# Giving the depthwise filters to an instruction order in units of five or three rounds instead of one

## The chip, the cores and the metric

The kernel runs on one NeuronCore of a Trainium2 chip. The metric is the device time in microseconds of one execution of the whole kernel (lower is better); the time of a kernel is the median of several executions.

## The reference

Four layers run one after the other on x of shape (32, 56, 56, 96), float32, images in the first dimension and channels last.

- Layer 0 makes per-image mixing weights of four experts (`rw = sigmoid(mean(x) @ Wr + br)`), expands 96 channels to 384 with a mixed 1x1 product, normalisation and relu, filters each of the 384 channels with a mixed 3x3 filter (again normalised, relu), projects to 96 channels, and adds the input.
- Layer 1 filters each of the 96 channels with its own 5x5 filter and adds the result to its input:

```
y = conv(x, kernel5x5, groups=96, padding='SAME')
x = x + y
```

- Layer 2 applies relu, then filters each channel with its own 3x3 filter, then takes a 96x96 product over channels with a bias and a normalisation:

```
y = relu(x)
y = conv(y, dw_kernel3x3, groups=96, padding='SAME') + dw_bias
y = (y @ pw_kernel + pw_bias) * inv + (beta - moving_mean * inv)
```

- Layer 3 is a Swin block: attention in shifted 7x7 windows (three heads of 32), with layer norm ahead, and a perceptron of width 384 with a second layer norm, each added to its input.

## The kernel before, in words

**Stages.** Each image passes through four stages: `stage_router` (layer 0's mixing weights), `stage_conditional` (the rest of layer 0), `stage_depthwise` (layers 1 and 2) and `stage_swin` (layer 3). In step s of the outer loop the stages of four images are recorded together: the router of image s, the conditional stage of s-1, the depthwise stage of s-2 and the Swin stage of s-3.

**Where the order comes from.** The stages are generators. They do not issue instructions; they record them as units of work (`Work`), one for each call on the recorder `chip`, or one for all calls inside a `with chip.together()` block. A generator's `yield n` says that n of the stage's total weight has been recorded (49 for the depthwise stage). `interleave` turns this into a due time (`chip.target`) for what follows: the stage's planned start plus its planned length times the share already recorded, with `PLAN["depthwise"] = (1.48, 1.13)` in units of images.

`Recorder.order` then simulates the five queues with a table of costs (`COST` and `cost`). When an engine is free it takes, of the units in its queue, the one with the earliest due time whose buffers are available; units that lack a buffer are passed over. A unit enters its queue when all that it depends on is done. The event that puts it there is handled after the engines were last asked, so when a unit on TensorE ends, its direct successor is not yet in the queue at the moment TensorE chooses again: if anything else can start, that goes first. If TensorE finds nothing for 250 ns, the planner gives it a filler, a product of the identity with itself (`chip.spare`; `banks<-ident` of 128x128 in the profile). The order found is issued as it is, on all engines, by `give`: this is line 500, and so nearly all instructions of the profile carry L500.

**Banks.** All products go to one ring of eight PSUM banks (`mm = cv = banks("banks", 8)`). A unit takes its banks when it starts; a bank comes free when its last user is done. A unit that starts a bank also waits for the buffers that the users of this bank write (for the second half of layer 2 that is `x3`, of which there is one).

**The depthwise stage.** `x1` holds the image as 128 partitions: 32 channels of a group are spread with four rows of the image each (`RB = 4`), three groups (`NG = 3`), and 14 blocks of four rows in the free dimension, padded to 60 columns. Filters are banded 32x32 matrices (`band5`, `band3`), so that a product of 32 rows by 32 columns of TensorE mixes eight channels with four rows each. A *round* is twelve such products, three groups by four quarters, each at its own place in the array. Layer 1 takes ten rounds for each half of the image, two row blocks (m = 0, 1) by five columns (d = 0 to 4); layer 2 takes six for each half, two row blocks by three columns. All rounds of a half add up in three banks. The halves of layer 1, and the first of layer 2, have 7 blocks (392 columns); the second half of layer 2 has 8 (448 columns).

After a half of layer 1, ScalarE writes `x2` from the three banks with relu (`x<-banks` in the profile). After a half of layer 2, ScalarE copies the banks to `x3`, and DMAs bring it into `filtered` in natural order. Then eight units of products with `pw` (`banks<-pw,filtered`) make the tokens of the Swin stage (`res`).

**Other units named below.** `banks<-xT,wmix`: expansions of layer 0. `banks<-h,wmix`: its projections. `h<-h,mix,h`: its filter taps on VectorE. `banks<-ident,lnd`: transposes of normalised tokens in the Swin stage; `lnd` is made by GpSimd, as are `tb` and `var`. `banks<-hT,w` and `banks<-w,hid`: the perceptron's two products. `banks<-exps,ones`, `banks<-exps,v`, `banks<-wo,oT`, `banks<-slots,wq` and the like: attention.

Of the kernel before, what the change touches and what calls it, by code (L numbers as in the profile page):

```python
# [36 lines left out]
NG = 3  # L37
NQ = 4
# [465 lines left out]
def kernel(  # L504
# [82 lines left out]
    for at, name in (  # L587
# [4 lines left out]
        src = a[name]  # L592
        if len(src.shape) == 1:
            src = src.rearrange("(o m) -> o m", o=1)
        elif len(src.shape) == 4:
            src = src.rearrange("e a b m -> (e a b) m")
# [8 lines left out]
    for at, name in (  # L605
# [4 lines left out]
        src = a[name]  # L610
        if len(src.shape) == 1:
            src = src.rearrange("(o m) -> o m", o=1)
        elif len(src.shape) == 4:
            src = src.rearrange("a b o m -> (a b o) m")
# [143 lines left out]
    chip = Recorder(nc)  # L758
# [174 lines left out]
    def stage_depthwise(b, res):  # L933

        def lines(t):

            return t.rearrange("(c r) m w -> c r m w", r=RB)

        x1 = chip.new(x1s)
        x2 = chip.new(x2s).part(0, 1)
        filtered = chip.new(filtereds).part(0, 1)

        xT = added.pop(b).rearrange("c (m r w) -> c r m w", r=RB, w=W)
        for g in range(NG):
            gs = slice(32 * g, 32 * g + 32)
            half = RB // 2
            for to, r, m in ((half, 0, 0), (0, half, 1)):
                for k in range(half):  # L950
                    chip.sync.dma_start(
                        out=lines(x1[:, g, m : m + NBLK, 2 : 2 + W])[:, to + k], in_=xT[gs, r + k]
                    )
        yield 6


        def tiles(banks, weights, src, first, n, dx, back):

            for t in range(2 * dx):
                m, d = divmod(t, dx)  # L960
                with chip.together():
                    for g in range(NG):
                        for q in range(NQ):
                            other = (q - g if back else q + g) % NQ
                            qs, os = slice(32 * q, 32 * q + 32), slice(32 * other, 32 * other + 32)
                            chip.tensor.matmul(
                                banks[g][os, : n * W].rearrange("p (m w) -> p m w", w=W),
                                weights[qs, g, t],
                                src[qs, g, first + m : first + m + n, d : d + W],
                                start=(t == 0),  # L970
                                stop=(t == 2 * dx - 1),
                            )
                yield 1

        for u in range(2):
            banks = [chip.new(cv) for _ in range(NG)]
            n = NBLK // 2
            yield from tiles(banks, band5, x1, n * u, n, 5, False)
            for g in range(NG):
                chip.scalar.activation(  # L980
                    x2[:, g, 1 + n * u : 1 + n * (u + 1), 1 : 1 + W].part(u),
                    banks[g][:, : n * W].rearrange("p (m w) -> p m w", w=W),
                    AF.Relu,
                )


        for first, n in ((0, NBLK // 2), (NBLK // 2, NBLK // 2 + 1)):
            banks = [chip.new(cv) for _ in range(NG)]
            half = int(first > 0)
            yield from tiles(banks, band3, x2.part(*range(half + 1)), first, n, 3, True)  # L990
            x3 = chip.new(x3s)
            for g in range(NG):
                pc = banks[g][:, : n * W].rearrange("p (m w) -> p m w", w=W)
                chip.scalar.copy(x3[:, g, :n, : W - 3], pc[:, :, 3:])
                chip.scalar.copy(x3[:, g, :n, W - 3 :], pc[:, :, :3])
            for g in range(NG):
                gs = slice(32 * g, 32 * g + 32)
                src = lines(x3[:, g])

                m = max(first, 1)  # L1000
                last = min(first + n, NBLK)
                into = filtered.part(half)
                dst = into[gs, RB * (m - 1) : RB * (last - 1)].rearrange("c (m r) w -> c r m w", r=RB)
                for r in range(RB):
                    chip.sync.dma_start(out=dst[:, r], in_=src[:, r, m - first : last - first])
                for r in range(1, RB) if first == 0 else (0,):
                    chip.sync.dma_start(out=into[gs, H - RB + r], in_=src[:, r, 0 if r else NBLK - first])

        for i in range(NROW):
            tokens = filtered.part(*((0,) if i < 3 else (0, 1))).rearrange("c r w -> c (r w)")  # L1010
            pt = chip.new(mm)
            if i % 2 == 0:
                res.append(chip.new(ress))
            into, n = chunk(res, i)
            with chip.together():
                for j in range(n):
                    at = LT * (NL * (i // 2) + i % 2 * 4 + j)
                    chip.tensor.matmul(
                        pt[:LT, j * CM : (j + 1) * CM],
                        tokens[:, at : at + LT],  # L1020
                        pw,
                        start=True,
                        stop=True,
                    )
            chip.scalar.copy(into.rearrange("p j c -> p (j c)"), pt[:LT, : n * CM])
            yield 1
            if i == 2:
                yield 3
# [8 lines left out]
    def chunk(res, i):  # L1037

        return (parts(res, i, 4, NL), NL - 4) if i % 2 else (parts(res, i, 0, 4), 4)
# [527 lines left out]
```

## Time and profile before

| | |
|---|---|
| time, median of 3 runs | 5202.46 us (5202.14 to 5204.24) |
| span of the profiled execution, first to last instruction | 5212.6 us |
| the profiled execution's time outside this span | not given |
| mean granted TensorE clock | 0.985 |
| TensorE matmul records, busy | 58578, 5050.6 us (97%) |
| of these filter products (`banks<-x,band`) | 24576, 856.3 us |
| VectorE busy | 4300.9 us (83%) |
| ScalarE busy | 3836.9 us (74%) |
| GpSimd busy | 3028.8 us (58%) |

PE is TensorE, DVE VectorE, ACT ScalarE, POOL GpSimd, SP the engine that issues the DMAs. A product in float32 is two matmul records, so one round of twelve products appears as 24 records ("x24") and a run of five rounds as x120. In a timeline line the columns are the start, the time from first start to last end, the engine, the line, the operation, its tiles, its shape and the number of records; successive units of the same form are merged. Matmuls are pipelined and the ends are modelled, so the time a unit takes from TensorE is read from its start to the start of the next unit.

### The profile page before, as it was taken

To read this page: it belongs to the slowest core of one execution; us is meant where nothing else is said; L and a number is where in the kernel's file an instruction comes from. 1 tells how busy PE (TensorE), PEld (TensorE's weight loads), DVE (VectorE), ACT (ScalarE), POOL (GpSimd) and SP (SyncE) were. 2 spreads that over 40 slices of the span, in tenths; PEclk is the share of its full clock that TensorE was granted. 3 is DMA by queue.
4 is the path that set the end of the run, shared out by engine and by line. 5 is a ranking of instruction groups with operands and counts; after the bars stand their busy time and mean duration, and the time that the engine had idled before them with its cause. 6 is when DMAs were issued, how large, how long until landed. Compare 5 with 4: busy or idle time off the path is not lost.

```text
span 5212.6 us, 139630 instructions
## 1 busy us (share of the span) xinstructions
PE 5050.6 (97%) x58578; PEld 3343.9 (64%) x58578; DVE 4300.9 (83%) x5561; ACT 3836.9 (74%) x7649; POOL 3028.8 (58%) x2432
## 2 busy tenths in 40 slices
PE   5789999999999999999999999999999999999999
PEld 4556666666666666666666666666666666666677
DVE  7877988888888888888888888888888888888722
ACT  3457778877778777777877777877777877777755
POOL 5455766565665556666555665656576555566533
PEclk9899999999999999999999999999999999999999
DMA  1111101111111111111111111111111111110110
GB/s 43 23 28 37 38 18 32 33 39 36 39 21 30 31 39 36 39 23 30 33 35 37 37 30 26 30 36 38 37 35 22 32 33 39 36 39 21 23 28 19
DMA packets 482577, 166.34 MB, mean 32 GB/s; under 512 B 477951, under 2 KB 478612, under 8 KB 478868
## 3 DMA queue, kind: packets, MB, share of 16 engines
q1 hardware_dynamic: 481940, 157.33, 14.8%
q8 instruction: 463, 7.59, 0.6%
q14 instruction: 174, 1.43, 0.1%
HBM read 41.60 MB, written 38.54 MB: 15 GB/s over the span
## 4 chain that ended last, share of the span: by engine, by line
PE 74%; POOL 10%; DVE 5%; ACT 5%; issue 4%; DMA 1%; SPq 0%; ACTq 0%; DVEq 0%; POOLq 0%
PE banks L500 74%; DVE h L500 3%; POOL tb L500 3%; POOL lnd L500 2%; POOL xT L500 2%; ACT exps L500 2%; POOL exps L500 2%; POOL var L500 1%; ACT hid L500 1%; ACT h L500 1%; DMA out<-tb 1%; DVE wmix L500 1%; DVE hid L500 1%; ACT slots L500 0%; DVE res L500 0%
## 5 line engine op out<-in xcount | busy, mean ns | idle before, releaser
L500 DVE SCALAR_TENSOR_TENSOR h<-h,mix,h 128x784 f32<-128x784 f32 x3072 | 3309.6, 1113 | 71.1 <-ACT h L500 54.0
L500 POOL TENSOR_TENSOR var<-var,mhalf 112x4 f32<-112x4 f32 (+1 forms) x512 | 775.2, 1519 | 426.3 <-DVE var L500 419.6
L500 PE MATMUL banks<-x,band 32*32 32x392 f32 x24576 | 856.3, 510 | 0.0
L500 POOL TENSOR_TENSOR xT<-y,xT 96x392 f32<-96x392 f32 x256 | 470.2, 1838 | 445.5 <-ACT y L500 444.1
L500 PE MATMUL banks<-xT,wmix 96*128 96x448 f32 (+1 forms) x1536 | 697.9, 553 | 0.5 <-DVE wmix L500 0.5
L500 ACT ACTIVATE h<-h,biasd,s 128x784 f32<-128x784 f32 x384 | 398.9, 1039 | 366.1 <-DVE h L500 366.0
L500 ACT ACTIVATE hid<-banks,c 128x448 f32<-128x448 f32 (+1 forms) x768 | 436.5, 582 | 288.3 <-PE banks L500 279.9
L500 POOL TENSOR_TENSOR tb<-res 112x384 f32<-112x384 f32 (+1 forms) x256 | 476.4, 1866 | 286.7 <-DMA out<-tb 196.7
L500 PEld LDWEIGHTS banks<-w,hid 128*112 128x112 f32 x5376 | 584.7, 183 | 82.0 <-issue 37.8
L500 PE MATMUL banks<-hT,w 96*128 96x448 f32 (+1 forms) x1536 | 615.6, 502 | 0.2 <-DVE tb L500 0.2
L500 POOL TENSOR_TENSOR lnd<-res,var 112x384 f32<-112x384 f32 (+1 forms) x512 | 594.8, 1168 | 32.8 <-PE banks L500 16.2
L500 ACT ACTIVATE h<-banks,bias,s 128x448 f32<-128x448 f32 (+1 forms) x768 | 538.6, 709 | 91.0 <-PE banks L500 85.4
L500 PE MATMUL banks<-w,hid 128*112 128x96 f32 x5376 | 593.1, 267 | 7.4 <-ACT hid L500 6.4
L500 PE MATMUL banks<-h,wmix 128*96 128x392 f32 x1536 | 557.7, 501 | 15.7 <-ACT h L500 15.7
L500 PEld LDWEIGHTS banks<-x,band 32*32 32x32 f32 x24576 | 404.7, 103 | 250.9 <-issue 165.9
L500 ACT ACTIVATE exps<-banks 49x196 f32<-49x196 f32 x1536 | 506.2, 330 | 40.2 <-PE banks L500 15.3
L500 POOL TENSOR_TENSOR exps<-exps,keep_column 49x147 f32<-49x147 f32 x224 | 207.1, 925 | 480.8 <-ACT exps L500 427.4
L500 PEld LDWEIGHTS banks<-h,wmix 128*96 128x96 f32 x1536 | 244.1, 165 | 256.8 <-issue 209.2
L500 PEld LDWEIGHTS banks<-xT,wmix 96*128 96x128 f32 x1536 | 261.2, 192 | 200.7 <-issue 95.5
L500 DVE TENSOR_REDUCE var<-lnsq 112x4 f32<-112x388 f32 (+1 forms) x512 | 253.1, 497 | 157.6 <-POOL lnd L500 118.1
L500 ACT ACTIVATE h<-h,mix 128x784 f32<-128x784 f32 x384 | 364.5, 949 | 18.0 <-POOL h L500 10.1
L500 PEld LDWEIGHTS banks<-hT,w 96*128 96x128 f32 x1536 | 256.4, 190 | 144.9 <-issue 74.8
(132 smaller groups left out, 7460.2 us busy)
## 6 DMA issues: line engine op xcount, KB each, us to landing
xT<-in_x SPq DMA_DIRECT2D x32, 1176.0 KB
x<-xT SPq DMA_DIRECT2D x384, 98.0 KB
out<-tb SPq DMA_DIRECT2D x128, 168.0 KB
filtered<-x SPq DMA_DIRECT2D x384, 49.0 KB
filtered<-x SPq DMA_DIRECT2D x384, 42.0 KB
out<-tb SPq DMA_DIRECT2D x128, 126.0 KB
filtered<-x SPq DMA_DIRECT2D x384, 7.0 KB
wpw<-in_L_conv_Wpw SPq DMA_DIRECT2D x1, 576.0 KB
```

The costliest lines, as they stand in the source:

```text
L500: getattr(getattr(self.nc, w.engine), method)(*args, **kw)
```

## The change

`tiles`, the function that records the filter products of one half of an image, no longer closes a unit after each round. It makes one unit for each row block m, holding all its rounds: five for layer 1, three for layer 2 (60 or 36 products). The products, their operands and their sequence are the same. The generator yields 5 or 3 after such a unit where it yielded 1 after each round, so the due times of all that follows are as before; the second and later rounds of a unit come under the due time of its first.

```diff
         def tiles(banks, weights, src, first, n, dx, back):
 
-            for t in range(2 * dx):
-                m, d = divmod(t, dx)
+            for m in range(2):
                 with chip.together():
-                    for g in range(NG):
-                        for q in range(NQ):
-                            other = (q - g if back else q + g) % NQ
-                            qs, os = slice(32 * q, 32 * q + 32), slice(32 * other, 32 * other + 32)
-                            chip.tensor.matmul(
-                                banks[g][os, : n * W].rearrange("p (m w) -> p m w", w=W),
-                                weights[qs, g, t],
-                                src[qs, g, first + m : first + m + n, d : d + W],
-                                start=(t == 0),
-                                stop=(t == 2 * dx - 1),
-                            )
-                yield 1
+                    for t in range(m * dx, (m + 1) * dx):
+                        d = t - m * dx
+                        for g in range(NG):
+                            for q in range(NQ):
+                                other = (q - g if back else q + g) % NQ
+                                qs, os = slice(32 * q, 32 * q + 32), slice(32 * other, 32 * other + 32)
+                                chip.tensor.matmul(
+                                    banks[g][os, : n * W].rearrange("p (m w) -> p m w", w=W),
+                                    weights[qs, g, t],
+                                    src[qs, g, first + m : first + m + n, d : d + W],
+                                    start=(t == 0),
+                                    stop=(t == 2 * dx - 1),
+                                )
+                yield dx
 
         for u in range(2):
             banks = [chip.new(cv) for _ in range(NG)]
```

## The prediction

> **What bounds the kernel now.** I read the page's engine and chain lines first, then TensorE's waits, then the timeline at the places where the filters run.
>
> ```profile
> PE 5050.6 (97%) x58578; PEld 3343.9 (64%) x58578; DVE 4300.9 (83%) x5561; ACT 3836.9 (74%) x7649; POOL 3028.8 (58%) x2432
> PE 74%; POOL 10%; DVE 5%; ACT 5%; issue 4%; DMA 1%; SPq 0%; ACTq 0%; DVEq 0%; POOLq 0%
> PE banks L500 <- POOL lnd L500: 51.3, 45, 2.8
> PE banks L500 <- ACT h L500: 47.4, 16, 5.4
> L500 PE MATMUL banks<-ident 128*128 128x128 f32 x1672 | 242.5, 288 | 39.9 <-ACT h L500 29.0 <-ACT y L500 10.0 <-ACT slots L500 0.4
> ```
>
> TensorE carries 74% of the chain that ended last and idles 3%, a third of it ahead of the first image. The third and fourth lines (total us, times, longest) are the large waits inside the loop. The last line is the planner's filler, an identity product given out when nothing else can start: two records each. Counted by stretches of 155 us it is 20 records an image in the steady part, 10 products of 0.29 us; the rest lies at head and tail. So in steady state TensorE loses about 3 us an image to filler and 2 us to waits: **TensorE's own work sets the pace**, and what counts is how long its units take in the order given.
>
> Now the filter products (a record is half an fp32 product, so one round of 12 is x24):
>
> ```profile
> 2482.90 1.02 PE L500 MATMUL banks<-x,band 32*32 32x448 f32 x24
> 2483.85 1.02 PE L500 MATMUL banks<-xT,wmix 96*128 96x448 f32 x2
> 2484.80 1.02 PE L500 MATMUL banks<-x,band 32*32 32x448 f32 x24
> ...
> 2511.61 14.20 PE L500 MATMUL banks<-x,band 32*32 32x392 f32 x480
> 2525.74 1.02 PE L500 MATMUL banks<-xT,wmix 96*128 96x448 f32 x2
> ...
> 2547.25 2.62 PE L500 MATMUL banks<-x,band 32*32 32x392 f32 x72
> 2549.80 0.49 PE L500 MATMUL banks<-ident,lnd 112*96 112x112 f32 x3
> ...
> 2622.13 0.92 PE L500 MATMUL banks<-xT,wmix 96*128 96x448 f32 x2
> 2622.89 0.91 PE L500 MATMUL banks<-hT,w 96*128 96x448 f32 x2
> ...
> 2676.83 0.83 PE L500 MATMUL banks<-wo,oT 97*112 97x97 f32 x6
> 2677.59 9.93 PE L500 MATMUL banks<-x,band 32*32 32x392 f32 x336
> 2687.45 2.21 PE L500 MATMUL banks<-h,wmix 128*96 128x392 f32 x6
> 2689.59 0.92 PE L500 MATMUL banks<-x,band 32*32 32x392 f32 x24
> ```
>
> Subtract starts. A lone round costs 0.95 us at 8 rows of blocks (448 columns), and 0.85 at 7. Three in a row cost 2.55 (2549.80 - 2547.25), no less than three lone ones. Fourteen cost 9.86, twenty 14.13: 0.70 each. Inside a run the rounds start 0.67 us apart and the last takes 1.20, so **a run of three or more costs 0.67 a round plus 0.55**, a lone one 0.67 plus 0.18. The unit before pays too: an expansion of 448 columns takes 0.76 (2622.89 - 2622.13) ahead of a full-array unit, 0.95 (2484.80 - 2483.85) ahead of a filter round.
>
> In the trace's records I count 468 runs of filter products in 32 images, 415 of them single rounds. In steady state images alternate. An even image has layer 1 as one run of 20, then 4 runs of layer 2's first half (1, 1, 1, 3 rounds) and 6 single rounds of the second: 11 runs. An odd one has layer 1 as 3 single, one of 14, 3 single, then 12 single rounds: 19.
>
> The planner explains this. When a round ends, its successor enters the queue only after TensorE has chosen again, so anything else that can start goes between. In a run of 20 the "anything else" is the other half of layer 1: the halves alternate and hold six of eight banks. The six evacuations x<-banks confirm it: all start from 2525.7 on, after the run. In the odd image the second half got its three banks only after three rounds: 3, then 7+7=14, then 3.
>
> **What the Trainium skill says.** TensorEngine Tiling (Array Packing), Key Properties: changing the tiling mode, not just the tile, drains TensorE. The trace agrees: between full-array units the next starts 0.16 us before the modelled end of the last; around a 32x32 run 0.07. TensorE: Matmul & The Clock Gate, Part 3 (The mechanism) says matmuls start and end in program order[...]. Perfetto Trace Analysis, Optimization Strategy, says repeated gaps can mean too few buffers to start the next tile; the fillers fit this only loosely.
>
> **The change part by part.** The products, weights and their sequence inside an accumulation stay: 24,576 records, the same evacuations, copies and DMAs. Nothing is added on any queue, SP's and POOL's included; the costs of these edits are nothing by count. What changes is that a unit is 60 or 36 products, nothing gets between its rounds, and the later rounds of a unit carry the first one's due time.
>
> 1. *Layer 1, even images.* After the first five rounds the planner stands where it stood after one: the other half is overdue and has its banks, or so I assume. I take the run of 20 as kept: 0. If it falls apart into four: 4 x (5 x 0.67 + 0.55) = 15.5 against 14.1, 1.4 an image worse.
>
> 2. *Layer 1, odd images.* Now 6 x 0.85 + 9.86 = 14.96. After: a five, something else, then fifteen: 3.88 + 10.54 = 14.42. Gain 0.54 x 16 images = 8.7 us. Bounds: 14.1 as one run, 15.5 as four.
>
> 3. *Layer 2.* Three lone rounds 2.55 or 2.83, a unit of three 2.55 or 2.83: nothing in themselves.
>
> 4. *Fewer switches.* After: even 1 + 2 + 2 = 5 runs, odd 2 + 2 + 2 = 6; over 16 pairs 176, so 292 fewer. What the unit ahead pays, from medians with a filter behind against a full-array unit behind: expansion 448 columns 0.18 (91 times), 392 columns 0.18 (31), hT,w 0.17 (59), pw,filtered 0.09 (127; taken from wo,oT, of the same shape), wo,oT 0.09 (42), the rest 0.02 to 0.17. Weighted 0.125 us. 29 of 468 runs are followed by another small mode, where the switch stays: 0.117. **292 x 0.117 = 34 us.**
>
> 5. *Waiting behind a longer unit.* A unit that becomes ready now waits up to 3.9 us in layer 1, 2.5 or 2.8 in layer 2, where it waited under 1 beside lone rounds and 10 to 14 beside the long runs. Behind it are queued the expansions that feed ACT's h and VectorE's taps, and the transposes and products of attention. Cover: even now ACT's only short of work and POOL is busy 0.15 of 14.4 us in the run of 20, and the image's time survives it. I take 0; bounds -1.4 us an image (banks free earlier, half the fillers go) and +2.9 (fillers double).
>
> Sum on TensorE: 34 + 9 = 43 us. It counts where TensorE is on the chain. Over two images (2480 to 2800 us) the chain is 80% TensorE; it lies on ACT and POOL from 2561 to 2591 and on POOL from 2607 to 2626, and the filter runs lie outside both stretches. What is saved before a POOL stretch can return as a longer wait for lnd, though. I credit 85%: 37 us. The durations are those of the profiled execution, whose span, 5212.6, is 10 us over the median of the runs; no other time of that execution is given. 37 of 5212.6 is 0.7%, and 5202.5 - 37 gives **5166**.
>
> **Rivals.**
>
> *No change (about 5206).* Layer 1 falls into four units with others between in every image: even +1.4 and 3 switches more, odd +0.55 and 3 fewer: 16 x 1.95 = +31. Layer 2 alone gives 14 fewer runs a pair: 16 x 14 x 0.117 = -26. Net +5. For it: the planner's rule that a successor is never at hand. Against: two overdue halves fill each other's gap now.
>
> *Slower (about 5246).* The long unit holds TensorE when an attention product or expansion becomes ready; its ACT, VectorE and POOL steps start later, and the image later has nothing for TensorE: fillers and waits for lnd. Price: 10 more fillers an image, 2.9 us, over 30 images 87, less 43 is +44. It decides from 43/30 = 1.4 us an image, five fillers or half a unit of lost time once. For it: POOL's tb, var, lnd stretch already stops TensorE 2.7 us in one image of two, and a new order lands elsewhere in all of these. Against: the run of 20 is a longer block than any unit here.
>
> *Faster still (about 5125).* Layer 2 holds three banks for some 6 us a half where it held them for about 10, and x3 with them; half the fillers go, 1.4 x 30 = 42 us more.
>
> **How the numbers follow.** Main case 0.50, faster still 0.10, no change 0.15, slower 0.25. Differences within 0.2% (10 us) are about what a measurement of this kernel cannot tell from none. Faster 0.60, same 0.15, slower 0.25. The range, 5130 to 5240, leaves out about half of the fastest case and a little of the slow one. For the main case alone: 5145 to 5188.
>
> **What would show it.** x24 runs all but vanish: the filter runs become x72 and x120 or multiples, about 176 of them. A lone x72 costs 2.55 or 2.83, a lone x120 3.88. Expansions are 0.76 more often. The identity row stays near 1672 and waits for lnd near 51 us. I am wrong if layer 1 shows four x120 runs an image (no change), or if fillers and waits rise by over 1.4 us an image (slower).

## The result, and the profile after

The changed kernel takes 5919.14 us (median of 4 runs, 5912.66 to 5926.2) against 5203.2 us before (5202.14 to 5204.24): 716 us more, ratio 1.1376 with a 95% interval of 1.136 to 1.1392. The execution that was profiled took 5912.66 us; its span is 5910.9 us, its mean granted TensorE clock 0.929.

The page of the changed kernel: the engine line, the chain that ended last, VectorE's filter taps, the filter products and the planner's filler (busy us, mean ns of one | idle before, releaser).

```profile
PE 5321.9 (90%) x59518; PEld 3741.5 (63%) x59518; DVE 4205.9 (71%) x5561; ACT 3850.4 (65%) x7649; POOL 3225.6 (55%) x2432
PE 63%; POOL 15%; DVE 9%; issue 9%; ACT 2%; DMA 1%; SPq 0%; POOLq 0%; ACTq 0%; DVEq 0%
L500 DVE SCALAR_TENSOR_TENSOR h<-h,mix,h 128x784 f32<-128x784 f32 x3072 | 3242.3, 1093 | 589.0 <-ACT h L500 581.1
L500 PE MATMUL banks<-x,band 32*32 32x392 f32 x24576 | 777.7, 501 | 5.1 <-issue 3.1
L500 PE MATMUL banks<-ident 128*128 128x128 f32 x2612 | 406.0, 297 | 49.7 <-ACT y L500 25.2
```

TensorE's share of the chain fell from 74% to 63%. Span less TensorE's busy time was 162.0 us before and is 589.0 now: 427 of the 698 us by which the span grew are idle time. The other 271 are busy time: fillers +163.5 (406.0 less 242.5), filter products -78.6 (777.7 against 856.3 us), and some 187 us in which the rest of the same work ran slower. The clock is enough to explain that: (1 - 0.929) x 5910.9 = 420 us of full clock are missing, against (1 - 0.985) x 5212.6 = 78. Laid over TensorE's busy time in the two traces, 315 us of this fall within it now and 69 did before, 245 more; the rest is lost while TensorE idles, where it costs nothing further. VectorE's taps wait 581.1 us for ACT's h now; in the kernel before, the wait was (total us, times, longest):

```profile
DVE h L500 <- ACT h L500: 54.0, 34, 17.3
```

TensorE's waits after (total us, times, longest):

```profile
PE banks L500 <- POOL lnd L500: 429.3, 84, 14.5
PE banks L500 <- ACT h L500: 72.6, 42, 6.2
```

The wait for GpSimd's `lnd` was 51.3 us with a longest of 2.8. It now holds most of the new idle time, in pieces of up to 14.5 us.

TensorE's timeline after, one image (start, us, engine, line, operation and tiles, records, wait ahead):

```profile
2549.11 0.79 PE L500 MATMUL banks<-ident,lnd 112*96 112x112 f32 x3 [3.94 <-POOL lnd L500]
...
2562.73 5.15 PE L500 MATMUL banks<-x,band 32*32 32x448 f32 x144
2567.81 2.40 PE L500 MATMUL banks<-pw,filtered 97*112 97x97 f32 x22
...
2612.17 0.92 PE L500 MATMUL banks<-ident,lnd 112*96 112x112 f32 x4 [5.13 <-POOL lnd L500]
2623.70 0.80 PE L500 MATMUL banks<-ident,lnd 112*96 112x112 f32 x3 [7.07 <-POOL lnd L500]
...
2644.70 16.05 PE L500 MATMUL banks<-x,band 32*32 32x392 f32 x552
2661.10 2.62 PE L500 MATMUL banks<-x,band 32*32 32x392 f32 x72
2663.65 1.04 PE L500 MATMUL banks<-qT,kT 32*113 32x98 f32 x24
...
2678.61 0.31 PE L500 MATMUL banks<-wr,pooled_w 96*128 96x4 f32 x2
```

The filters did bunch, more than predicted: all twenty rounds of layer 1 and three of layer 2 are one run (x552), and the second half of layer 2 is one run of six rounds (x144), now in the middle of the perceptron instead of at its end. Counted in the records, 468 runs became 113. The loss is elsewhere: two waits for `lnd` at the start of the next attention, 12 us together, and one of 3.9 us in the perceptron.

All engines at the second of these waits:

```profile
2612.62 9.54 DVE L500 SCALAR_TENSOR_TENSOR h<-h,mix,h 128x784 f32<-128x784 f32 x10
2612.89 10.13 POOL L500 TENSOR_TENSOR xT<-y,xT 96x392 f32<-96x392 f32 x1
2622.98 0.66 POOL L500 TENSOR_TENSOR lnd<-res,var 112x288 f32<-112x288 f32 x1
2623.70 0.80 PE L500 MATMUL banks<-ident,lnd 112*96 112x112 f32 x3 [7.07 <-POOL lnd L500]
2625.78 1.75 PE L500 MATMUL banks<-xT,wmix 96*128 96x448 f32 x2
2627.47 1.84 PE L500 MATMUL banks<-qT,kT 32*113 32x98 f32 x24
2634.20 1.72 PE L500 MATMUL banks<-xT,wmix 96*128 96x448 f32 x2
2637.70 5.96 DVE L500 SCALAR_TENSOR_TENSOR h<-h,mix,h 128x784 f32<-128x784 f32 x6 [15.54 <-ACT h L500]
```

An add on GpSimd (median 1.4 us over its 256 executions) starts 0.27 us after a row of ten VectorE taps and takes 10.13 us: it ends 0.86 us after the row does. `lnd` stands behind it on GpSimd, the transposes behind `lnd` on TensorE, and behind these, in order, the two expansions that were to feed ACT's h. The first takes 1.69 us to the next start (2627.47 - 2625.78) where one took 0.76 or 0.95 before, since TensorE's clock stands at half from 2619.1 to 2636.2; the second starts only at 2634.20. So VectorE, which held GpSimd up, has no taps for 15.54 us. The Trainium skill, SBUF — State Buffer, Who interferes with whom, states that a VectorE instruction with two SBUF inputs contends with a GpSimd instruction that reads SBUF, and calls the contention an exclusive lock. The trace agrees in kind; here the add waited out the whole row of ten, not one instruction.

DMA traffic, which is high in the first of the windows below, is a rival that the trace rules out. Of the 31 such adds that take over 8 us, all lie under taps for at least 99% of their time, and 6 have next to no DMA beside them; 4 that take under 2 us have a DMA share over 0.4.

Windows over the same stretch (sum, then busy us and count of PE, PEld, DVE, ACT, POOL; granted clock; DMA share; GB/s):

```profile
2601.00:2621.00 20.00, 9.38 (x33) 5.34 (x31) 19.28 (x23) 7.64 (x12) 16.39 (x4) 0.87 0.55 114
2621.00:2641.00 20.00, 17.30 (x123) 12.19 (x125) 4.46 (x6) 11.17 (x26) 7.10 (x7) 0.62 0.00 0
```

In 40 us TensorE idles 13.3 us and loses 0.13 x 20 + 0.38 x 20 = 10.2 us more to the clock. VectorE is full in the first window and nearly empty in the second.

The second change of order is in layer 0. The mixing weights of the next image (the router) need one small TensorE product and then a chain of short VectorE operations. TensorE and VectorE before, at that product and at the last operation of the chain:

```profile
2384.14 0.31 PE L500 MATMUL banks<-wr,pooled_w 96*128 96x4 f32 x2
```

```profile
2416.76 0.27 DVE L500 TENSOR_SCALAR bias<-bias,s,t 96x1 f32<-96x1 f32 x1
```

and VectorE after:

```profile
2740.47 0.29 DVE L500 TENSOR_TENSOR prod<-experts,rw 128x132 f32<-128x132 f32 x1
2741.62 0.28 DVE L500 TENSOR_REDUCE mix<-prod 128x33 f32<-128x132 f32 x1
...
2746.59 0.27 DVE L500 TENSOR_SCALAR bias<-bias,s,t 96x1 f32<-96x1 f32 x1
2746.78 1.02 DVE L500 SCALAR_TENSOR_TENSOR h<-h,mix,h 128x784 f32<-128x784 f32 x1
...
2752.51 10.00 DVE L500 SCALAR_TENSOR_TENSOR h<-h,mix,h 128x784 f32<-128x784 f32 x9 [3.52 <-ACT h L500]
```

Matching the recorded order with the trace gives which image each belongs to. Before, the weights were ready at 2417, the taps of the image ahead ran until 2453, and the next image's began at 2441: stages overlapped by 12 us. After, the input of the small product is ready at 2655.4 and the product runs at 2678.6, behind the filter runs and a row of attention units (23 us, where it waited 7 before). Its VectorE chain then ends at 2746.9, where the last tap of the image ahead begins (2746.78). From the product to that end it takes 68 us, where it took 33 before, so the larger part of the delay arises on VectorE, among the taps. The next image's taps begin at 2753. The stages no longer overlap: 176 us of taps and 5 of gap make 181 us an image, against some 155. Of these 26 us, 17 are the overlap that is gone (12 and 5), and 9 are a longer tap stage (176 us against 163 and 171 in turn).

### The profile page after: what moved, and what is told of

Same layout as the page of the kernel before. It is cut to its first block, busy times and chain, and to the rows that moved or that the text cites. A ratio compares the mean times of both kernels' runs of the same rounds, so it can differ in the third digit from the quotient of the medians.

```text
span 5910.9 us, 141223 instructions
## 1 busy us (share of the span) xinstructions
PE 5321.9 (90%) x59518; PEld 3741.5 (63%) x59518; DVE 4205.9 (71%) x5561; ACT 3850.4 (65%) x7649; POOL 3225.6 (55%) x2432
## 4 chain that ended last, share of the span: by engine, by line
PE 63%; POOL 15%; DVE 9%; issue 9%; ACT 2%; DMA 1%; SPq 0%; POOLq 0%; ACTq 0%; DVEq 0%
PE banks L500 63%; DVE h L500 7%; POOL xT L500 5%; POOL var L500 4%; POOL lnd L500 3%; POOL tb L500 2%; DMA out<-tb 1%; POOL exps L500 1%; ACT h L500 1%; DVE hid L500 1%; DVE tb L500 1%; DVE wmix L500 0%; ACT exps L500 0%; DVE var L500 0%; DVE oT L500 0%
## 5 line engine op out<-in xcount | busy, mean ns | idle before, releaser
L500 DVE SCALAR_TENSOR_TENSOR h<-h,mix,h 128x784 f32<-128x784 f32 x3072 | 3242.3, 1093 | 589.0 <-ACT h L500 581.1
L500 POOL TENSOR_TENSOR xT<-y,xT 96x392 f32<-96x392 f32 x256 | 716.0, 2798 | 405.3 <-ACT y L500 403.1
L500 PE MATMUL banks<-x,band 32*32 32x392 f32 x24576 | 777.7, 501 | 5.1 <-issue 3.1
L500 PE MATMUL banks<-ident,lnd 112*96 112x112 f32 x1792 | 287.7, 286 | 429.3 <-POOL lnd L500 429.3
L500 PEld LDWEIGHTS banks<-x,band 32*32 32x32 f32 x24576 | 544.8, 103 | 174.5 <-issue 79.8
L500 PEld LDWEIGHTS banks<-ident,lnd 112*96 112x96 f32 x1792 | 210.1, 138 | 598.8 <-POOL lnd L500 473.2
L500 POOL TENSOR_TENSOR tb<-res 112x384 f32<-112x384 f32 (+1 forms) x256 | 348.8, 1367 | 375.0 <-DMA out<-tb 234.2
L500 PEld LDWEIGHTS banks<-ident 128*128 128x128 f32 x2612 | 384.8, 212 | 130.1 <-issue 48.6
L500 ACT ACTIVATE slots<-banks,c 96x392 f32<-96x392 f32 (+2 forms) x384 | 208.2, 581 | 384.2 <-PE banks L500 384.0
L500 PE MATMUL banks<-ident 128*128 128x128 f32 x2612 | 406.0, 297 | 49.7 <-ACT y L500 25.2
```

Of the source, the lines that this page charges most:

```text
L500: getattr(getattr(self.nc, w.engine), method)(*args, **kw)
```

## The experiments

Four theories. A: the long units are harmless, the new order is the culprit. B: a long unit blocks TensorE's queue by its length, in any order. C: rows of taps catch GpSimd's instructions, and TensorE waits behind them. D: the router comes too late, and the stages of neighbouring images stop overlapping. Ratios are to the kernel before on the same chip.

**The old order, rounds brought together at issue.** The planner plans single rounds as before. `mates` lists the rounds of one row block; when the first is issued, the others follow at once.

```diff
+    def gathered(self, found):
+        for w in found:
+            mates = getattr(w, "mates", (w,))
+            if w is mates[0]:
+                yield from mates
...
-            for w in self.order():
+            for w in self.gathered(self.order()):
...
+            mates = [], []
...
+                mates[m].append(chip.work[-1])
+                chip.work[-1].mates = mates[m]
```

> The planner works on single rounds as before and its order is kept; only when the order is issued are the five or three rounds of a row block brought together, at the place of the first. Theory A (a new order of the whole kernel is what costs): the units are as long as in the changed kernel but the order round them is the one of before, so the time is 5203 less the saved switches, 5150 to 5190 us, with waits for lnd near 51 us and fillers at 1672 records. Theory B (a long unit in itself starves the other engines): slower than before by hundreds of us, 5450 to 5900, with waits for lnd over 200 us.

5309.41 us, 1.0207 (1.0187 to 1.0226). The records show 175 filter runs, and the units ahead of filters did get cheaper: pw,filtered 201.8 to 185.3 us, hT,w 579.8 to 572.8, xT,wmix, w,hid and wo,oT some 5 us each, 39 in all (from start to start, waits included). Yet the time rose by some 104 us. TensorE's waits in this run, its timeline at one, and the chain of waits into it:

```profile
PE banks L507 <- POOL exps L507: 72.2, 26, 5.7
PE banks L507 <- POOL lnd L507: 58.9, 60, 2.8
```

```profile
2548.54 1.53 PE L507 MATMUL banks<-exps,ones 113*32 113x392 f32 x6 [5.18 <-POOL exps L507]
```

```profile
2537.61 9.74 POOL xT L507
...
2547.43 1.07 POOL exps L507
...
2548.54 58.25 PE banks L507 x916
```

Here `exps` stands behind an add that the taps have held up, 9.74 us. The wait is 5.18 us, and from its middle on TensorE's clock stays at half for 13.65 us. So both expectations failed: long units at their old places are not free, as A expected, nor do they cost hundreds of us, as B did. Of the 716 us this explains 104 at most.

**One layer alone, and due times alone.** The first run has units of five in layer 1 only; the second has units of three in layer 2 (`size = 3 if dx == 3 else 1`); the third keeps single rounds and gives all of a row block the due time of the first (`size = 1`, `yield 0 if (t0 + 1) % dx else dx`).

```diff
-            for t in range(2 * dx):
-                m, d = divmod(t, dx)
+            size = 5 if dx == 5 else 1
+            for t0 in range(0, 2 * dx, size):
                 with chip.together():
+                    for t in range(t0, t0 + size):
+                        m, d = divmod(t, dx)
...
-                yield 1
+                yield size
```

> Units of five for layer 1, single rounds for layer 2. Theory A: part of the loss, 5250 to 5500 us; the two halves of layer 1 no longer alternate with single rounds and the order settles into another cycle. Theory B: most of the loss lies here, since the 3.9 us units are the longest: 5650 or more.

> Single rounds for layer 1, units of three for layer 2. Theory A: part of the loss, 5250 to 5550 us, the more so if it is layer 2's interleaving that kept TensorE in work while VectorE ends a conditional stage. Theory B: little, 5200 to 5300, since units of 2.5 us are short.

> Single rounds as before, but all rounds of a row block come under the due time of its first, as in the changed kernel. Theory A: the order changes by the due times alone, 5230 to 5450 us. Theory B: no unit is longer than before, so 5190 to 5220.

Layer 1 alone: 5438.9 us, 1.0447 (1.0419 to 1.0474). Layer 2 alone: 5673.99, 1.0898 (1.0875 to 1.0921). Due times alone, with not one long unit: 5374.95, 1.0324 (1.0303 to 1.0344). Any of these plans the kernel anew, and each new plan is worse. All three speak against B: units of five rounds cost 233 us, the shorter units of three 468, and single rounds under new due times 169. Layer 2 alone does more harm than layer 1, with its router late in the same way (ready at 2682 while the taps of the image ahead end at 2683).

**The caught add moved.** The add into `xT` is issued on VectorE instead of GpSimd at its old place in the order: in the changed kernel, in the gathered one, and in the kernel before as a control.

```diff
+        self.issuer = None
...
-                    getattr(getattr(self.nc, w.engine), method)(*args, **kw)
+                    getattr(getattr(self.nc, w.issuer or w.engine), method)(*args, **kw)
...
+            chip.work[-1].issuer = "vector"
```

> The changed kernel with its planned order; only when it is issued, the add of y to xT (256 instructions) goes to VectorE's queue in place of GpSimd's. Theory C (a GpSimd instruction that is caught behind a run of VectorE's taps takes some 10 us, the normalised tokens or probabilities that TensorE waits for are queued behind it, and each such wait is followed by microseconds at half clock): in the changed kernel one xT add an image is caught so, so the waits for lnd fall from 429 to under 200 us, the clock that is lost halves, and the time falls to 5500 to 5700 us. It cannot come back to 5203, since the order itself has 940 more filler records. Theory B (long units starve the engines whatever GpSimd does): above 5850.

> The order of before with the rounds of a row block brought together at issue (run e1), and the add of y to xT on VectorE's queue. Theory C: the wait of 5.2 us for exps in one image of two goes (72 us to under 15) and with it its 13.7 us at half clock, so about 100 us come back and the switches saved show at last: 5150 to 5220 us. Theory B: the long units cost by themselves, 5290 or more.

> Control: the kernel before with the same add on VectorE's queue. Only 6 of its 256 xT adds took over 4 us, so theory C expects little: 141 us more work on VectorE, spread, against less on GpSimd; 5150 to 5240 us. If it falls as far as e6 does against e1, the add has nothing to do with the units' length.

Changed: 5941.16 us, 1.1434 (1.1395 to 1.1473). Gathered: 5410.46, 1.0397 (1.038 to 1.0414). Before: 5435.77, 1.0447 (1.0429 to 1.0464). The control shows that the move costs some 230 us itself, so the first run cannot clear the add; but its waits for `lnd` stay at 386.2 us, and in its place 52 of the `lnd` instructions take over 4 us (25 in the changed kernel, 15 in the kernel before). It fits that whatever GpSimd has next is caught, not this add alone. The wait for `exps` was expected to go too. In the gathered kernel with the add moved it stays, and the control has one as well. The gathered one first, then the control:

```profile
PE banks L508 <- POOL exps L508: 71.6, 41, 5.3
PE banks L501 <- POOL exps L501: 62.7, 31, 5.2
```

With the add moved in both, gathering takes 25 us off. The saving of switches shows where the two kernels compared pay nearly the same waits.

**Units of two in layer 2** (`size = 1 if dx == 5 else 2`).

> Layer 2 in units of two rounds, layer 1 in single rounds. If a unit's length is what costs (theory B), units of two lie between single rounds (5206) and units of three (5674): 5300 to 5550. If what costs is which order the planner falls into (theory A), length orders nothing and pairs may be as slow as threes or slower: 5600 or more.

5557.35 us, 1.068 (1.0658 to 1.0701): between the kernel before and units of three, which neither theory marked off well. It tells little.

**The router earlier.** Only the planned start and length of the router's stage change, so that its units get earlier due times: in the changed kernel, in the kernel before as a control, in the control's order gathered, and in the changed kernel by 0.06 of an image only.

```diff
-PLAN = {"router": (-0.14, 1), ...
+PLAN = {"router": (-0.4, 0.8), ...
```

> The changed kernel with one line of the plan edited: the router stage's due times start 0.4 images ahead, over 0.8 images, where they started 0.14 ahead over 1. Theory D (in the changed kernel the next image's mixing weights, which need one small product on TensorE and a few short VectorE instructions, come only when the last taps of the image before end, so the tap stages of two images no longer overlap and the period is a whole tap stage and a start): the weights are ready over 20 us ahead of the end of the taps, the period falls from 181 to 160 to 170 us and the time to 5250 to 5480. Theory B (long units starve the engines): above 5850, since the units are the same.

> Control: the kernel before with the router's due times 0.3 images ahead, over 0.8. Its mixing weights are ready 34 us ahead of the end of the taps already, so theory D expects no such change: 5120 to 5260 us. If it falls by hundreds of us, the router's lateness was a cost of both kernels and not what the change brought.

> The order of e10 with the rounds of a row block brought together when it is issued. What bringing them together is worth by itself, in a second order: by the switches saved 37 us under e10; with a wait for a GpSimd instruction as in e1 (5309 against 5206), up to 100 us over it. Under e10 by 15 to 45 us if the wait of e1 was an accident of that order.

> The changed kernel with the router's due times 0.2 images ahead where they were 0.14, over 1 image as before: a shift of 0.06 images, some 10 us. Theory D: once the router's product is ahead of the backlog the cycle breaks, so a small shift does most of it: 5300 to 5600 us. If the loss were in proportion to the router's lateness, a third of e9's gain at most: 5700 or more.

The control and its gathered form have (-0.3, 0.8), the last (-0.2, 1). Changed: 5637.38 us, 1.0832 (1.0814 to 1.085), so 282 of the 716 us are gone. Control: 5312.96, 1.0201 (1.018 to 1.0223); in the old kernel a like edit costs 106. By a bit: 5661.87, 1.0873 (1.0851 to 1.0895), already 257 of the 282 us. What counts is whether the weights come before the taps of the image ahead end, not by how much; in the first of these runs stages overlap by 10 to 18 us again, and VectorE's taps wait far less for ACT's h than the 581.1 us of the changed kernel:

```profile
DVE h L500 <- ACT h L500: 103.1, 41, 8.3
```

D holds for a part; the expected 5250 to 5480 us were not reached. The order and the trace together show why no more came back: the taps of one image now take 173 to 191 us, so the period falls only from 181 to some 172. Gathering the control's order gives 5267.65, 45 less: the switches' saving a second time.

What is left in the changed kernel with the early router, TensorE's waits and the timeline of all engines:

```profile
PE banks L500 <- POOL lnd L500: 318.6, 56, 11.7
```

```profile
2525.15 12.11 POOL L500 TENSOR_TENSOR xT<-y,xT 96x392 f32<-96x392 f32 x2
2525.16 9.54 DVE L500 SCALAR_TENSOR_TENSOR h<-h,mix,h 128x784 f32<-128x784 f32 x10
...
2541.73 0.98 PE L500 MATMUL banks<-ident,lnd 112*96 112x112 f32 x4 [11.66 <-POOL lnd L500]
```

Much the same picture as with the router late: ten taps, two adds of which the first takes 10.4 us of the 12.11, `var` and `lnd` behind them, and TensorE 11.66 us behind `lnd`.

**Fewer taps.** The order stays; four of the nine taps of layer 0's filter are left out at issue, which shortens the rows of taps. In the changed kernel, in the kernel before, and in the changed kernel with the early router.

```diff
+                if w.left_out:
+                    continue
...
+                    chip.work[-1].left_out = t % 2 == 0
```

> The changed kernel in its planned order, with four of the nine taps of layer 0's filter (those of even number but the first) left out of VectorE's queue; the rest is issued as it was. If the loss is VectorE's tap chain and the GpSimd instructions caught behind it (theories C and D), TensorE's waits nearly vanish and the time is its own work: 5090 less or more fillers, 5080 to 5250 us, within 100 us of e14. If long units starve the engines by themselves (theory B), most of the distance to e14 stays, 400 us or more.

> Control: the kernel before with the same four taps left out. It waits little as it is, so only little is to be had: 5080 to 5200 us by all theories.

> The changed kernel with the router's due times of e9 and four of the nine taps left out as in e13. If the late router and the GpSimd instructions caught behind the taps are the whole loss, the long units run at about the time of e14 (5015): 4980 to 5080 us, with waits for lnd under 60 us. If long units cost by themselves, 5200 or more remain.

Changed: 5350.98 us, 1.0275 (1.0245 to 1.0305). Before: 5015.45, 0.9631 (0.9612 to 0.965). Changed with early router: 5021.86, 0.9649 (0.9632 to 0.9666). The distance to the kernel before shrinks from 716 to 336, and with the early router to 6. TensorE's waits and filler in the first of these, then in the last:

```profile
PE banks L503 <- POOL lnd L503: 87.2, 27, 6.1
```

```profile
L503 PE MATMUL banks<-ident 128*128 128x128 f32 x2612 | 375.1, 283 | 0.7 <-ACT slots L503 0.4 <-ACT exps L503 0.3
```

```profile
PE banks L503 <- POOL lnd L503: 20.1, 18, 2.1
```

```profile
L503 PE MATMUL banks<-ident 128*128 128x128 f32 x1804 | 259.6, 282 | 0.7 <-ACT slots L503 0.4
```

With the router early and the taps fewer, long units cost nothing that shows. The clock says the same: 0.957 in the first, 0.999 in the last, 1.0 in the kernel before with fewer taps. Leaving out taps also takes work from VectorE, so the 380 us are the price of long, full rows of taps in this order, not of the contention alone. Nor are they separate shares: the router alone gives 282, after the taps it gives 329.

**Gathering by part.** The first experiment's edit for layer 1 alone (`if dx == 5`), for layer 2 alone (`if dx == 3`), and for all but the second half of layer 2 (`if dx == 5 or first == 0`).

> The order of before with only layer 1's rounds brought together when it is issued. By switches: some 5 us from own time and 6 from fewer switches, 5185 to 5205 us; if the wait for exps of e1 (5309) comes from this layer, 5250 to 5320.

> The order of before with only layer 2's rounds brought together when it is issued. By switches: some 25 us, 5165 to 5190; if the wait for exps of e1 comes from this layer, 5250 to 5320.

> The order of before with the rounds brought together when it is issued, in layer 1 and in the first half of layer 2 alone; the second half's rounds stay single. In the image where e1 waits 5.2 us for exps, the second half of layer 2 is what was brought together shortly before, so without it that wait should be small: by switches 8 to 25 us under before, 5180 to 5198. If the wait is still there, 5280 or more.

Layer 1: 5206.02 us, 0.9997 (0.9989 to 1.0006); layer 2: 5327.92, 1.023 (1.0213 to 1.0247); without the last half: 5187.96 (5178.24 to 5203.36), 0.997 (0.9961 to 0.998). Layer 2 alone has the long wait of the first experiment:

```profile
PE banks L507 <- POOL exps L507: 72.8, 26, 5.7
```

Layer 1 alone ends where it began. The last one is faster than both kernels, by 0.3%, or some 16 us: it leaves single the half of layer 2 whose gathering moved `exps` behind the taps, and its waits for `lnd` and fillers are near those of the kernel before (56.3 us and 241.6, against 51.3 and 242.5).

## Why the prediction was wrong

*Steps 1 and 2, the rounds of layer 1.* Right in their assumption and better than that: 29 of 32 images have all twenty rounds in one run, the odd ones too, where 5 and 15 were forecast. From start to start the filter products take 774.8 us, 824.7 before: 50 us saved.

*Step 3, layer 2.* Right: a lone x72 takes 2.54 or 2.82 us, a lone x120 takes 3.88.

*Step 4, fewer switches.* Right in count where the order is kept (175 runs for 176). In size it was of the right order where no new wait eats it: gathering all takes off 25 and 45 us in two orders, for a forecast of 34, with 9 more for step 2 and 37 credited; without the last half it takes off 16, for layer 1 alone nothing, and in the kernel before it adds 104. In the changed kernel there are only 113 runs.

*Step 5, "Waiting behind a longer unit ... I take 0; bounds -1.4 us an image ... and +2.9".* This step failed, and with it the path: the prediction let TensorE's own work set the pace in the new order too. With the forecast saving added, the rest of the change costs (716 + 37) / 32 = 23.5 us an image. Three things were wrong in it.

- It priced waits in the old order. The due times of units ahead and behind stayed, but the queue is planned unit by unit, and a bigger unit moves all that follows. The single rounds with the first one's due time, no unit longer, already cost 3.2%, some 170 us.
- Its cover was read off one stretch: that ACT is short of work and GpSimd idle beside the run of 20 says nothing on the small product of the router, which has to come well before the taps of the image ahead end. With 16 us more of waiting ahead of it, and with its VectorE chain stretched to the end of the taps, it took the overlap of neighbouring images away. Given earlier due times, the router gives back 257 to 282 us.
- It priced a wait by its length. A wait of TensorE of some us brings a stretch at half clock, so part of it is paid again: 427 us of new idle time came with 245 us of clock lost within the busy time.

*The credit of 85%*, for what returns as a longer wait for `lnd`, had the right place and no size: that wait went from 51.3 to 429.3 us. The prediction even showed the stretch where GpSimd's chain stops TensorE 2.7 us, and took it as a constant. Its list of the stretches where the chain leaves TensorE lacks a third, from 2747.8 to 2762.3; no filter run starts there either, so its sum does not change.

*The rivals.* "Slower" had the right mechanism: long units in the way, ACT, VectorE and GpSimd later, an image later fillers and waits for `lnd`. It gave 10 more fillers an image; there are (2612 - 1672) / 2 / 32 = 15 more. The term that was mis-sized is the wait itself, which it left out of its sum of 87 us: new idle time and clock are 427 and 245 us. The sign that it named came true: fillers and waits for `lnd` rose by 17 us an image ((163.5 + 378.0) / 32), not by 1.4. Layer 1 did not fall apart, so "no change" failed by its own sign; "faster still" expected half the fillers.

*Left open.* Which of the planner's choices makes layer 2's units send the router to the end was not separated; for layer 2 due times alone change nothing in the plan. That the second half of layer 2 moved from the perceptron's end to its middle, and so no longer covers the start of the next attention, is read from the two timelines and only argued. The contention was not taken away with all taps in place: moving one add left the waits nearly as they were, so how much of the 716 us the caught GpSimd instructions cost by themselves is argued, not shown. The plan's start times were also left as they stood for single rounds. Every new plan tried lost 106 us or more, that of the old kernel with its router earlier among them; whether other start times would suit long units was not tried.

## What to carry to other kernels

Where a planner makes the order, changing a unit's size changes the whole order, and the edit's own cost, here forecast at 43 us and found at 16 to 45 in the orders where it paid, says little: regroup in the old order at issue first, and take the new plan as a second change. Ask of each small unit that others depend on (here two records of TensorE an image) what now stands ahead of it, and how late it may be. Price a wait of an engine with its successors' waits and with the clock that it costs, not by its length alone.

## What the runs showed of the hardware

- **The clock falls at shorter waits than the page's window.** The Trainium skill, TensorE: Matmul & The Clock Gate, Part 1, names an idle window of about 3.4 us after which the clock halves. In the kernel before, 17 of the 19 waits of TensorE from 2.5 to 3 us met a stretch at half clock, of 3.4 or 6.8 us; in the changed kernel 2 of 40 waits from 0.8 to 2 us did. With fewer taps, 24 waits of 3.24 us each met 10 to 31 us at half clock, and the changed kernel, which has 134.3 us of TensorE idle in its span (5336.4 - 5202.1 busy), lost 0.043 x 5336.4 = 229 us of clock: more than it idled.
- **A row of VectorE taps can keep GpSimd out for its whole length.** An add of 96x392 elements that takes 1.4 us in the median took 10.13 us behind ten taps back to back. In the gathered kernel one took 9.73: it starts in the sixth of seventeen taps and ends in the sixteenth, which starts 0.1 us late. It is not always so: in the changed kernel 25 adds ran in under 2 us beside a tap that followed at once on the one before it, and that tap took some 1.8 us in place of 1.0. What decides between the two is not shown.
- **Small products pay for a change to the 32x32 filters too.** The units of pw,filtered have products only 97 columns wide. At full clock their last record takes 0.19 us to the next start ahead of a filter run and 0.10 ahead of other work, the 0.09 that the prediction took from wo,oT. In the gathered kernel 80 such places are gone (47 for 127): 7.5 of the 16.5 us saved there. A shorter wait is 1.7 more and half clock some 3; the rest is not accounted for.
